# A selective-scan block with a feed-forward net: the decay's exponentials taken in one instruction over two PSUM banks

## The chip, the cores and the metric

The kernel runs on one core of one Trainium2 chip. A core has TensorE (PE, matrix products), VectorE (DVE), ScalarE (ACT), GpSimd (POOL) and SyncE (SP, which here issues the DMAs). Each engine works through its own queue in order; engines wait for one another by semaphores. TensorE writes its products to PSUM, which has eight banks of 2 KB per partition (512 float32 columns each).

The metric is the device time of one execution in microseconds (us), lower is better. The kernel before takes 2990.38 us, the median of three runs (2989.24 to 2991.91).

## The reference

x is (2, 1024, 512). A selective state-space layer with state size 128 for each of the 512 channels, a residual and a layernorm, then a gated feed-forward net of width 2048, a residual and a layernorm. Cut to what matters:

```python
xn = x * rsqrt(mean(x * x, -1) + 1e-06) * norm_w
xn = xn * sigmoid((xn @ select_proj_w.T + select_proj_b) * select_gate)
delta, B_ssm, C_ssm = split(xn @ x_proj_w.T)            # 128 each
delta = softplus(delta @ dt_proj_w.T + dt_proj_b)
A = -exp(A_log)                                          # (512, 128)
def step(h, inp):                                        # over 1024 tokens
    dt, bt, ct, xt = inp
    h = exp(dt[:, :, None] * A) * h + (dt * xt)[:, :, None] * bt[:, None, :]
    return h, einsum('bdn,bn->bd', h, ct)
x = layernorm(x + (ys + x * D_param) @ out_proj_w.T)
x = layernorm(x + (silu(x @ w_gate.T) * (x @ w_up.T)) @ w_down.T)
```

The recurrence over tokens is the core of it: for each token, channel and state a decay exp(dt A) and an input dt x B.

## The kernel before, in words

**Tiling.** The 2048 tokens are cut into 64 groups of 32 tokens (`st`). In each, the 512 channels are done in two halves (`h = 2 st + i`, 128 of them), and each half in eight rounds (`r`, lines 636 to 698) of 32 channels. So there are 1024 rounds `k`. States lie on the 128 partitions. A round's tile is 128 x 32 x 32: 32 channels of 32 tokens each, 1024 columns, two PSUM banks.

**One round.** TensorE makes two tiles with four matmuls, each with a contraction of 32 rows that stand in a quarter of the array of its own:

- `bu` (line 658, two matmuls, one bank each): the products dt x B of round k. The pool `ps_bu` has two buffers of two banks.
- `a` (line 391, in `decay_mm`, two matmuls): the exponents dt A, made one round ahead, for round k + 1. Each matmul has a tile of one bank, and the pool `ps_a` has two of them. They are issued alternately with those of `bu`: bu, a, bu, a.

ScalarE takes the exp of the exponents into `a_sb` (line 398, in `decay_exp`), for columns 1 to 31 of each channel, so 16 x 31 = 496 columns for each of the two banks. Column 0 of `a_sb` stays zero; that restarts the scan at each channel. For this ScalarE also copies the state carried over from the group before, with the first token's input added to it, into column 0 of `bu` (line 669, 32 columns; called the first tokens' copy here). `a_sb` holds three rounds.

VectorE runs the recurrence in one scan over the 1024 columns (line 674) from `a_sb` and `bu` into `hs[h]`. The scan needs the exp of its round, which was made one round before, and the copy of its own round.

**The order in a round.** The order of each engine is written out by hand. In a round of the loop: first `work.others()`, which issues what ScalarE, VectorE, GpSimd and SyncE have to do for the layers around the scan; then bu, a, bu, a; then on ScalarE the first exp, the copy, the second exp; then the scan; then what is called TensorE's side group here:

- `y_round` (line 410): products of the states with C for the half before. Rounds 1, 4 and 7 of a half have three, three and two of these, by the list `ROUNDS` (line 21).
- `work.tensor()`: one step of a generator for the next tokens' projections (`pre`), the output projection (`post`) or the feed-forward net (`ffn`). A step is mostly one matmul 128 x 256 with a contraction of 128. The list `PARTS` (line 22) gives each round a credit of 4, 3 or none; unused credit is kept up to 6. If no step is ready in the written order, `work.tensor()` returns False and the side group of that round ends there.

So the length of the side groups varies, and it is fixed when the program is built. After the side group GpSimd gets the next inputs of the matmuls (`diag`, lines 362 and 372) and the parts of the carried state (`carry_a`, `carry_h`).

**What waits for what around the change.** The matmul of `a` in round k + 1 writes the bank that an exp of round k reads, so it waits for this exp. `bu` of round k + 2 uses the banks of `bu` of round k, so it waits for scan k. TensorE's queue is in order: what is behind a waiting matmul waits too.

Of the kernel before, what the change touches and what calls it, by code (L numbers as in the profile page):

```python
# [9 lines left out]
FP = mybir.dt.float32  # L10
AF = mybir.ActivationFunctionType
ALU = mybir.AluOpType
PSUM = bass.MemoryType.PSUM
DRAM = bass.MemoryType.DRAM

P = 128
S = 32
# [3 lines left out]
ROUNDS = ((), (0, 1, 2), (), (), (3, 4, 5), (), (), (6, 7))  # L21
PARTS = (4, 0, 3, 3, 0, 3, 3, 0)
# [12 lines left out]
def kernel(  # L35
# [17 lines left out]
    nc = tc.nc  # L53
# [50 lines left out]
    a_t = main.tile([P, NM, N], FP, name="a_t")  # L104
# [7 lines left out]
    a_sb = main.tile([P, 3, 32, S], FP, name="a_sb")  # L112
# [8 lines left out]
    ps_y = tc.alloc_tile_pool(name="ps_y", bufs=1, space=PSUM)  # L121
    ps_m = tc.alloc_tile_pool(name="ps_m", bufs=1, space=PSUM)
    ps_bu = tc.alloc_tile_pool(name="ps_bu", bufs=2, space=PSUM)
    ps_a = tc.alloc_tile_pool(name="ps_a", bufs=2, space=PSUM)

    x_tr = x_t.rearrange("(k p) t -> p k t", p=P)
    first_xT = pre_pool.tile([P, NM, TC], FP, tag="xT", name="xT_0")
# [180 lines left out]
    def toks(st):  # L308
        return ts(st % SPC, S)

    prepared, carried, dus, ddts, hs, ys = {}, {}, {}, {}, {}, {}

    def load(st):


        ub = step_pool.tile([P, 2, P], FP, tag="ub", name=f"ub_{st}")
        rows = u_d[ts(st, S), :].rearrange("t (m g c) -> g t m c", g=4, c=32)
        for g in range(4):
            nc.sync.dma_start(
                ub[ts(g, S), 0, :].rearrange("t (m c) -> t m c", c=32), rows[g]  # L320
            )
            nc.sync.dma_start(ub[ts(g, S), 1, :], b_d[ts(st, S), :])
        prepared[st] = ub
        nc.gpsimd.tensor_copy(
            cz[st % 3][:, 28:284].rearrange("p (b w) -> p b w", w=32)[:, :, 0:4],
            made[st // SPC][2][:, toks(st)].rearrange("p (b t) -> p b t", t=4),
        )
        cd = step_pool.tile([P, D], FP, tag="cd", name=f"cd_{st}")
        cu = step_pool.tile([P, D], FP, tag="cu", name=f"cu_{st}")
        nc.sync.dma_start(cd, dt0_d[st : st + 1, :].to_broadcast([P, D]))  # L330
        nc.sync.dma_start(cu, u_d[st * S : st * S + 1, :].to_broadcast([P, D]))
        carried[st] = cd, cu
# [9 lines left out]
    def carry_h(st, i):  # L342

        if st % NSB == 0:
            return
        cd, cu = (t.rearrange("p (b i e) -> p b i e", i=2, e=16)[:, :, i, :] for t in carried[st])
        last = hs[2 * (st - 1) + i][:, :, S - 1].rearrange("p (b e) -> p b e", e=16)
        nc.gpsimd.tensor_tensor(cd, cd, last, ALU.mult)  # L348
        nc.gpsimd.tensor_tensor(cu, cu, cd, ALU.add)

    def diag(j, part):

        h, a = j // 2, 2 * (j % 2)
        if h >= 2 * NS:
            return
        st, i = divmod(h, 2)
        name, m = divmod(part, 2)
        shape = [P, 2, 16, S]
        if name == 0:
            if m == 0:  # L360
                ddts[j] = half_pool.tile(shape, FP, tag="ddt", name=f"ddt_{j}")
            nc.gpsimd.tensor_tensor(  # L362
                ddts[j][:, m, :, :],
                made[st // SPC][0][:, a + m, toks(st)].unsqueeze(1).to_broadcast([P, 16, S]),
                hot[:, ts(i, 16)].unsqueeze(2).to_broadcast([P, 16, S]),
                ALU.mult,
            )
        else:
            if m == 0:
                dus[j] = half_pool.tile(shape, FP, tag="du", name=f"du_{j}")  # L370
            uv = prepared[st][:, 0, :].rearrange("p (m i e) -> p m i e", i=2, e=16)[:, :, i, :]
            nc.gpsimd.tensor_tensor(  # L372
                dus[j][:, m, :, :],
                uv[:, a + m, :].unsqueeze(2).to_broadcast([P, 16, S]),
                hot.unsqueeze(1).to_broadcast([P, 16, S]),
                ALU.mult,
            )

    NG = NS * 16

    def place(k):
        h, r = divmod(k, 8)
        m, pair = divmod(r, 2)
        return h, m, pair

    def decay_mm(k, b):

        h, m, pair = place(k)
        g = 2 * pair + b
        ps = ps_a.tile([P, 16, S], FP, tag="a", name=f"a_{k}_{b}")  # L390
        nc.tensor.matmul(  # L391
            ps, a_t[ts(g, 32), m, :], ddts[k // 4][ts(g, 32), m % 2, :, :],
            start=True, stop=True,
        )
        return ps

    def decay_exp(k, b, ps):
        nc.scalar.activation(  # L398
            a_sb[:, k % 3, ts(b, 16), 1:], ps[:, :, 1:], AF.Exp
        )  # L400

    def y_round(h, b):


        st, i = divmod(h, 2)
        if i == 0 and b == 0:
            ys[st] = ps_y.tile([P, 512], FP, tag="y", name=f"y_{st}")
        at = 28 + 28 * b
        for m in range(NM):
            nc.tensor.matmul(  # L410
                ys[st][ts(m, 32), ts(i, 256)], cz[st % 3][:, at : at + 32],
                hs[h][:, ts(m, 64), ts(b, 4)],
                start=(i == 0 and b == 0), stop=(i == 1 and b == 7),
                skip_group_check=True,
            )

    def y_out(st):

        tt, s = divmod(st, 4)
        if s == 0:  # L420
            yrs[tt] = post_pool.tile([P, 4, P], FP, tag="yr", name=f"yr_{tt}")
        yc = post_pool.tile([P, P, 4], FP, tag="yc", name=f"yc_{st}")
        nc.scalar.copy(yc, ys.pop(st).rearrange("p (q t) -> p q t", t=4))  # L423
        nc.gpsimd.tensor_tensor(yc, yc, pick.unsqueeze(1).to_broadcast([P, P, 4]), ALU.mult)  # L424
        nc.gpsimd.tensor_tensor(yc[:, :, 0:2], yc[:, :, 0:2], yc[:, :, 2:4], ALU.add)
        nc.gpsimd.tensor_tensor(yrs[tt][:, s, :], yc[:, :, 0], yc[:, :, 1], ALU.add)
        if s == 3:
            work.add(post(tt), front=True)
# [191 lines left out]
    work = Work()  # L620
# [8 lines left out]
    for part in range(4):  # L629
        diag(0, part)  # L630
    diag(1, 0)
    for b in range(2):
        decay_exp(0, b, decay_mm(0, b))

    pres, credit = {}, 0
    for k in range(NG):
        h, m, pair = place(k)
        st, i = divmod(h, 2)
        r = k % 8
        work.others()  # L640
        if r == 0:
            hs[h] = half_pool.tile([P, 256, S], FP, tag="h", name=f"h_{h}")

            if i == 1 and st:
                y_out(st - 1)
            if i == 0:
                if st % SPC == 0 and st // SPC + 1 < NC:
                    pres[st // SPC + 1] = work.add(pre(st // SPC + 1), front=True)
                if st + 1 < NS:
                    if (st + 1) % SPC == 0:  # L650
                        work.finish(pres[(st + 1) // SPC])
                    load(st + 1)

        bu = ps_bu.tile([P, 32, S], FP, tag="bu", name=f"bu_{k}")
        nxt = []
        for b in range(2):
            g = 2 * pair + b
            nc.tensor.matmul(  # L658
                bu[:, ts(b, 16), :], prepared[st][ts(g, 32), 1, :],
                dus[k // 4][ts(g, 32), m % 2, :, :],  # L660
                start=True, stop=True,
            )
            if k + 1 < NG:
                nxt.append(decay_mm(k + 1, b))
        if nxt:
            decay_exp(k + 1, 0, nxt[0])
        h0 = carried[st][1].rearrange("p (b i e) -> p b i e", i=2, e=16)
        first = 4 * m + 2 * pair
        nc.scalar.copy(  # L669
            bu[:, :, 0].rearrange("p (b e) -> p b e", e=16), h0[:, first : first + 2, i, :]  # L670
        )
        if nxt:
            decay_exp(k + 1, 1, nxt[1])
        nc.vector.tensor_tensor_scan(  # L674
            hs[h][:, ts(r, 32), :].rearrange("p q t -> p (q t)"),
            a_sb[:, k % 3, :, :].rearrange("p q t -> p (q t)"),
            bu.rearrange("p q t -> p (q t)"),
            0.0, ALU.mult, ALU.add,
        )
        if h:  # L680
            for b in ROUNDS[r]:
                y_round(h - 1, b)
        credit = min(credit + PARTS[r], 6)
        while PARTS[r] and credit > 0 and work.tensor():
            credit -= 1

        j, r4 = divmod(k, 4)
        if r4 == 3:
            diag(j + 2, 0)
        else:  # L690
            diag(j + 1, r4 + 1)
        if r == 1:
            if i == 0 and st:
                carry_h(st, 1)
            if i == 1 and st + 1 < NS:
                carry_h(st + 1, 0)
        if r == 5 and i == 0 and st + 1 < NS:
            carry_a(st + 1)
# [81 lines left out]
```

## Time and profile before

| | |
|---|---|
| median of three runs | 2990.38 us |
| the profiled execution | 2998.38 us, its span 2996.6 us |
| mean granted TensorE clock | 0.973 of full speed |
| TensorE busy | 2808.5 us (94%) |
| VectorE busy | 2370.2 us (79%), 2313.3 of it in 1024 scans |
| ScalarE busy | 1697.1 us (57%), 1206.3 of it in 2048 exps of line 398 |
| GpSimd busy | 1928.4 us (64%) |
| DMA | 171.89 MB, 18.2% of 16 engines' span for the main queue |
| the loop of 1024 rounds | from about 92 to 2880 us of the span |

The profile is one execution. Busy time of TensorE counts matmuls, which overlap: the four of a round run together. The chain that ended last follows the work back from the last instruction, at each step to what released it. An entry in the table of waits says which engine, at which line, stood idle until which other instruction ended: total us, times, the longest. In the timeline the columns are the start in us from the start of the span, the duration, the engine, the line, the operation and its tiles. Each float32 matmul appears as two records, one behind the other.

### The profile page before, as it was taken

What the parts mean: (1) busy time and instruction counts of PE and PEld (TensorE: products, weight loads), DVE (VectorE), ACT (ScalarE), POOL (GpSimd) and SP (SyncE); (2) the same over time, 40 slices, a digit from 0 to 9 for tenths busy, and PEclk for the clock granted to TensorE, in tenths of its full rate; (3) what the DMA queues carried; (4) which work ended last, traced back from release to release, by engine and by line L of the source; (5) the groups of instructions that cost most, each with busy time, mean ns of one, the idle gap of its engine ahead of it and who ended that gap; (6) DMA issues with size and microseconds to landing.
All of it is one profiled execution on the core that took longest, in us unless ns stands there. A gap on an engine that the chain in (4) does not pass through costs nothing.

```text
span 2996.6 us, 53059 instructions
## 1 busy us (share of the span) xinstructions
PE 2808.5 (94%) x20672; PEld 1422.4 (47%) x20672; DVE 2370.2 (79%) x1184; ACT 1697.1 (57%) x4139; POOL 1928.4 (64%) x2094
## 2 busy tenths in 40 slices
PE   3798889999999999999999999999999999999988
PEld 2333334444444444444444444445444445454457
DVE  0589998888778888888888878888888888988840
ACT  2465566656465566665656546565656656565633
POOL 2465665767657676775666656767676757675734
PEclk7799999999999999999999999999999999999999
DMA  1101011212112121112202112111211212122124
GB/s 62 38 19 25 18 32 56 60 61 67 46 54 61 53 66 57 53 51 82 68 29 65 61 52 74 42 54 58 88 48 40 82 57 62 61 68 67 59 78 120
DMA packets 119673, 171.89 MB, mean 57 GB/s; under 512 B 47808, under 2 KB 70848, under 8 KB 119424
## 3 DMA queue, kind: packets, MB, share of 16 engines
q1 hardware_dynamic: 119424, 168.50, 18.2%
q8 instruction: 165, 2.70, 0.4%
q14 instruction: 84, 0.69, 0.1%
HBM read 158.87 MB, written 9.57 MB: 56 GB/s over the span
## 4 chain that ended last, share of the span: by engine, by line
PE 74%; DVE 13%; ACT 5%; issue 4%; POOL 3%; DMA 1%; SPq 0%; POOLq 0%; ACTq 0%; DVEq 0%
PE bu L658 26%; PE gu L514 15%; PE y L410 14%; DVE h L674 12%; PE d L532 7%; PE a L391 6%; PE op L457 2%; PE sel L181 2%; PE xp L181 1%; ACT a_sb L398 1%; ACT bu L669 1%; PE ss L195 1%; PE b L241 1%; POOL du L372 0%; POOL dt L305 0%
## 5 line engine op out<-in xcount | busy, mean ns | idle before, releaser
L674 DVE TENSOR_TENSOR_SCAN h<-a_sb,bu 128x1024 f32<-128x1024 f32 x1024 | 2313.3, 2280 | 520.3 <-ACT bu L669 515.0
L398 ACT ACTIVATE a_sb<-a 128x496 f32<-128x496 f32 x2048 | 1206.3, 591 | 1021.1 <-PE a L391 848.4
L391 PE MATMUL a<-ddt,a_t 32*128 32x512 f32 x4096 | 1307.1, 649 | 14.4 <-POOL ddt L362 13.4
L658 PE MATMUL bu<-du,ub 32*128 32x512 f32 x4096 | 1205.1, 647 | 49.8 <-DVE h L674 44.5
L362 POOL TENSOR_TENSOR ddt<-dt,hot 128x512 f32<-128x512 f32 x512 | 533.3, 1048 | 281.1 <-PE a L391 281.0
L372 POOL TENSOR_TENSOR du<-ub,hot 128x512 f32<-128x512 f32 x512 | 534.5, 1049 | 46.5 <-PE a L391 46.0
L658 PEld LDWEIGHTS bu<-du,ub 32*128 32x128 f32 x4096 | 338.7, 185 | 454.5 <-issue 280.9
L514 PE MATMUL gu<-x1T,w 128*128 128x256 f32 x2048 | 525.4, 399 | 20.2 <-DMA w<-in_wgu_s_dram 4.9
L410 PE MATMUL y<-h,cz 128*32 128x256 f32 x8192 | 530.5, 388 | 1.6 <-DVE h L674 1.6
L514 PEld LDWEIGHTS gu<-x1T,w 128*128 128x128 f32 x2048 | 373.3, 193 | 271.3 <-issue 183.1
L391 PEld LDWEIGHTS a<-ddt,a_t 32*128 32x128 f32 x4096 | 410.6, 185 | 56.0 <-ACT a_sb L398 34.2
L410 PEld LDWEIGHTS y<-h,cz 128*32 128x32 f32 x8192 | 229.5, 110 | 414.6 <-issue 304.3
L548 POOL TENSOR_SCALAR gu<-gu 128x256 f32<-128x256 f32 x128 | 108.4, 847 | 301.5 <-ACT gu L520 301.1
L532 PE MATMUL d<-w,hid 128*128 128x256 f32 x1024 | 260.9, 396 | 14.7 <-DVE x L538 6.9
L532 PEld LDWEIGHTS d<-w,hid 128*128 128x128 f32 x1024 | 185.0, 191 | 138.8 <-issue 98.5
L669 ACT COPY bu<-cu 128x32 f32<-128x32 f32 x1024 | 200.5, 196 | 1.4 <-PE bu L658 1.4
L424 POOL TENSOR_TENSOR yc<-yc,pick 128x512 f32<-128x512 f32 x64 | 66.5, 1039 | 165.4 <-ACT yc L423 165.4
L348 POOL TENSOR_TENSOR cd<-cd,h 128x256 f32<-128x256 f32 x124 | 106.4, 858 | 62.4 <-DVE h L674 62.4
L554 POOL TENSOR_TENSOR hid<-gu,e 128x256 f32<-128x256 f32 x128 | 93.0, 727 | 30.3 <-ACT e L553 27.9
L549 POOL TENSOR_TENSOR gu<-gu 128x256 f32<-128x256 f32 x128 | 94.3, 736 | 10.7
L520 ACT COPY gu<-gu 128x512 f32<-128x512 f32 x128 | 75.0, 586 | 45.8 <-PE gu L514 45.7
L538 DVE TENSOR_TENSOR x<-x,d 128x256 f32<-128x256 f32 x64 | 25.5, 399 | 94.9 <-PE d L532 94.9
(91 smaller groups left out, 1446.4 us busy)
## 6 DMA issues: line engine op xcount, KB each, us to landing
w<-in_wgu_s_dram SPq DMA_DIRECT2D x128, 512.0 KB, 4.6
w<-in_wd_s_dram SPq DMA_DIRECT2D x64, 512.0 KB, 4.1
cd<-dt_d SPq DMA_DIRECT2D x64, 256.0 KB, 3.8
cu<-u_d SPq DMA_DIRECT2D x64, 256.0 KB, 4.8
xT<-in_x_t_dram SPq DMA_DIRECT2D x8, 512.0 KB, 5.3
u_d<-uT SPq DMA_DIRECT2D x16, 256.0 KB, 2.0
ub<-u_d SPq DMA_DIRECT2D x256, 16.0 KB, 2.1
ub<-b_d SPq DMA_DIRECT2D x256, 16.0 KB, 1.9
```

Of the source, the lines that this page charges most:

```text
L348: nc.gpsimd.tensor_tensor(cd, cd, last, ALU.mult)
L362: nc.gpsimd.tensor_tensor(ddts[j][:, m, :, :], made[st // SPC][0][:, a + m, toks(st)].unsqueeze(1).to_broadcast([P, 16, S]), hot[:, ts(i, ...
L372: nc.gpsimd.tensor_tensor(dus[j][:, m, :, :], uv[:, a + m, :].unsqueeze(2).to_broadcast([P, 16, S]), hot.unsqueeze(1).to_broadcast([P, 16, ...
L391: nc.tensor.matmul(ps, a_t[ts(g, 32), m, :], ddts[k // 4][ts(g, 32), m % 2, :, :], start=True, stop=True,)
L398: nc.scalar.activation(a_sb[:, k % 3, ts(b, 16), 1:], ps[:, :, 1:], AF.Exp)
L410: nc.tensor.matmul(ys[st][ts(m, 32), ts(i, 256)], cz[st % 3][:, at : at + 32], hs[h][:, ts(m, 64), ts(b, 4)], start=(i == 0 and b == 0), s ...
L514: nc.tensor.matmul(ps[:, ts(a, TC)], w[:, a, k, :], x1T[:, k, :], start=(k == 0), stop=(k == NM - 1),)
L532: nc.tensor.matmul(ps[:, 0:HD], hid[:, f, ts(j, P)], w[:, f % 4, :], start=(f == 0), stop=(f == NH - 1),)
L548: nc.gpsimd.tensor_scalar_max(g, g, -80.0)
L658: nc.tensor.matmul(bu[:, ts(b, 16), :], prepared[st][ts(g, 32), 1, :], dus[k // 4][ts(g, 32), m % 2, :, :], start=True, stop=True,)
L669: nc.scalar.copy(bu[:, :, 0].rearrange("p (b e) -> p b e", e=16), h0[:, first : first + 2, i, :])
L674: nc.vector.tensor_tensor_scan(hs[h][:, ts(r, 32), :].rearrange("p q t -> p (q t)"), a_sb[:, k % 3, :, :].rearrange("p q t -> p (q t)"), b ...
```

## The change

The exponents `a` of a round come in one tile of two banks, and `ps_a` has one such tile instead of two of one bank: the same two banks. One exp of 32 x 31 = 992 columns takes the place of two of 496. Since it reads both banks, both matmuls of `a` of the next round wait for it.

The side group is now written ahead of the exp, the copy and the scan in the program, so that its length is known there; on TensorE's own queue the order stays. `size` counts its y rounds and its steps. With `size` below 3 the exp is issued ahead of the first tokens' copy, otherwise behind it.

```diff
-    ps_a = tc.alloc_tile_pool(name="ps_a", bufs=2, space=PSUM)
+    ps_a = tc.alloc_tile_pool(name="ps_a", bufs=1, space=PSUM)
...
-    def decay_mm(k, b):
+    def decay_mm(k, b, ps):
...
-        ps = ps_a.tile([P, 16, S], FP, tag="a", name=f"a_{k}_{b}")
         nc.tensor.matmul(
-            ps, a_t[ts(g, 32), m, :], ddts[k // 4][ts(g, 32), m % 2, :, :],
+            ps[:, ts(b, 16), :], a_t[ts(g, 32), m, :], ddts[k // 4][ts(g, 32), m % 2, :, :],
             start=True, stop=True,
         )
-        return ps
-
-    def decay_exp(k, b, ps):
-        nc.scalar.activation(
-            a_sb[:, k % 3, ts(b, 16), 1:], ps[:, :, 1:], AF.Exp
-        )
+
+    def decay_exp(k, ps):
+        nc.scalar.activation(a_sb[:, k % 3, :, 1:], ps[:, :, 1:], AF.Exp)
+
+    def decay_bank(k):
+        return ps_a.tile([P, 32, S], FP, tag="a", name=f"a_{k}")
...
-        nxt = []
+        nxt = decay_bank(k + 1) if k + 1 < NG else None
...
-            if k + 1 < NG:
-                nxt.append(decay_mm(k + 1, b))
-        if nxt:
-            decay_exp(k + 1, 0, nxt[0])
+            if nxt is not None:
+                decay_mm(k + 1, b, nxt)
+
+        size = 0
+        if h:
+            for b in ROUNDS[r]:
+                y_round(h - 1, b)
+                size += 1
+        credit = min(credit + PARTS[r], 6)
+        while PARTS[r] and credit > 0 and work.tensor():
+            credit -= 1
+            size += 1
+
+        if nxt is not None and size < 3:
+            decay_exp(k + 1, nxt)
         h0 = carried[st][1].rearrange("p (b i e) -> p b i e", i=2, e=16)
         first = 4 * m + 2 * pair
         nc.scalar.copy(
             bu[:, :, 0].rearrange("p (b e) -> p b e", e=16), h0[:, first : first + 2, i, :]
         )
-        if nxt:
-            decay_exp(k + 1, 1, nxt[1])
+        if nxt is not None and size >= 3:
+            decay_exp(k + 1, nxt)
         nc.vector.tensor_tensor_scan(
...
-        if h:
-            for b in ROUNDS[r]:
-                y_round(h - 1, b)
-        credit = min(credit + PARTS[r], 6)
-        while PARTS[r] and credit > 0 and work.tensor():
-            credit -= 1
```

More of the change, by code (lines that the diff above doesn't have):

```diff
@@ L631 @@
     diag(1, 0)
+    ps = decay_bank(0)
     for b in range(2):
-        decay_exp(0, b, decay_mm(0, b))
+        decay_mm(0, b, ps)
+    decay_exp(0, ps)
     pres, credit = {}, 0
```

## The prediction

> **What bounds the kernel now.** I read the page first: the busy shares and the chain that ended last.
>
> ```profile
> PE 2808.5 (94%) x20672; PEld 1422.4 (47%) x20672; DVE 2370.2 (79%) x1184; ACT 1697.1 (57%) x4139; POOL 1928.4 (64%) x2094
> ...
> PE 74%; DVE 13%; ACT 5%; issue 4%; POOL 3%; DMA 1%; SPq 0%; POOLq 0%; ACTq 0%; DVEq 0%
> ```
>
> TensorE carries three quarters of the chain, and ScalarE, whose instructions the change rewrites, one twentieth. So only that part of the change counts that lets TensorE start something sooner or later. Next the groups by line, for the three instruction kinds that move or set the moves:
>
> ```profile
> L674 DVE TENSOR_TENSOR_SCAN h<-a_sb,bu 128x1024 f32<-128x1024 f32 x1024 | 2313.3, 2280 | 520.3 <-ACT bu L669 515.0
> L398 ACT ACTIVATE a_sb<-a 128x496 f32<-128x496 f32 x2048 | 1206.3, 591 | 1021.1 <-PE a L391 848.4
> ...
> L669 ACT COPY bu<-cu 128x32 f32<-128x32 f32 x1024 | 200.5, 196 | 1.4 <-PE bu L658 1.4
> ```
>
> One scan, two exps and one copy per round, 1024 rounds. Then the table of waits:
>
> ```profile
> ACT a_sb L398 <- PE a L391: 848.4, 593, 9.5
> DVE h L674 <- ACT bu L669: 515.0, 603, 96.4
> ...
> PEld a L391 <- ACT a_sb L398: 34.2, 124, 1.0
> ```
>
> ScalarE mostly waits for TensorE, so its idle time is no cost. In 603 rounds VectorE stands idle until the first tokens' copy: the copy's place matters to the scan. The last line shows TensorE waiting for an exp, but only 34 us, because it counts a wait only while nothing else runs in TensorE. The timeline shows the rest. Here are a round with two y rounds as its side group, a round with two small steps, and the start of the next; columns are start, duration, engine, line:
>
> ```profile
> 1172.51 0.69 PE L658 MATMUL bu<-du,ub 32*128 32x512 f32 x1
> ...
> 1173.58 1.07 PE L410 MATMUL y<-h,cz 128*32 128x256 f32 x16
> 1173.71 0.60 ACT L398 ACTIVATE a_sb<-a 128x496 f32<-128x496 f32 x1 [4.64 <-PE a L391]
> ...
> 1174.20 0.20 ACT L669 COPY bu<-cu 128x32 f32<-128x32 f32 x1
> 1174.30 0.60 ACT L398 ACTIVATE a_sb<-a 128x496 f32<-128x496 f32 x1
> 1174.43 4.46 DVE L674 TENSOR_TENSOR_SCAN h<-a_sb,bu 128x1024 f32<-128x1024 f32 x2 [2.56 <-ACT bu L669]
> 1174.59 0.69 PE L658 MATMUL bu<-du,ub 32*128 32x512 f32 x1
> 1174.60 0.69 PE L391 MATMUL a<-ddt,a_t 32*128 32x512 f32 x1
> 1174.60 0.69 PE L658 MATMUL bu<-du,ub 32*128 32x512 f32 x1
> 1174.95 0.69 PE L391 MATMUL a<-ddt,a_t 32*128 32x512 f32 x1
> ...
> 1175.79 0.58 ACT L398 ACTIVATE a_sb<-a 128x496 f32<-128x496 f32 x1 [0.89 <-PE bu L658]
> 1176.01 1.13 PE L457 MATMUL op<-out_w,zT 128*128 128x256 f32 x4
> 1176.27 0.19 ACT L669 COPY bu<-cu 128x32 f32<-128x32 f32 x1
> 1176.38 0.59 ACT L398 ACTIVATE a_sb<-a 128x496 f32<-128x496 f32 x1
> ...
> 1177.07 0.69 PE L658 MATMUL bu<-du,ub 32*128 32x512 f32 x1
> ```
>
> A round starts with four matmuls (bu, a, bu, a) that run side by side within 20 ns of each other. The fourth of the second round does not: it starts at 1174.95, 0.36 late, 0.05 after the second exp of the round before ended (1174.30 + 0.60). Everything behind it on TensorE, here the op steps at 1176.01, is late by as much. Walking the timeline round by round, I find the last exp to be what TensorE waits for in 370 rounds, 206 us together (late fourth matmul plus late first one). That is the sum the change can work on. It sits in rounds after a short side group. I counted each round's units from the matmuls in it (one y round is 8 records, most steps are 2): 404 rounds have under three units, 126 of them the eighth round of a half with its two y rounds. They lie in 248 runs: 139 alone, 79 pairs, 30 longer ones. After a side group of three or more the exps are long done (in the usual round they end 2.38 after the round's start, and the next starts at 2.51 to 2.56).
>
> **What the Trainium skill says.** "ScalarE: Activation LUTs", section "What ACT_TABLE_LOAD costs", prices an activation with constant scale and bias at 186 ns plus 0.833 ns a column, and lets neighbours overlap by 93 ns. The trace agrees: 496 columns give 599 by that against 591 measured, and the copy starts 0.48 to 0.49 after an exp of 0.59, an overlap of about 0.11. "PSUM — Partial Sum Buffer", section "PSUM bank collisions raise a hardware error", wants two engines kept off one bank at once; hence each decay matmul waits for the exp that reads its bank, as at 1174.95. "TensorEngine Tiling (Array Packing)", section "Key Properties", has row tiles run independently: the four starts within 20 ns show it.
>
> **The change part by part.**
>
> *Two exps of 496 become one of 992.* Exps of 256 and 512 columns in the groups by line take 416 and 628 ns, so 0.83 ns a column; 587 (the usual duration of an L398) + 496 x 0.83 = 1.00 us. The skill's formula gives an estimate of 1.01. No row shows an exp across two banks: the ends I keep are 0.97 and 1.04.
>
> *Both decay matmuls now wait for that one exp.* Before, the first half's bank came free with the first exp. Now bu(0) starts and a, bu, a follow the exp. As the fourth matmul was the last anyway, a late exp costs the side group no more than before; where the exp was early it costs nothing. But the exp itself now needs the whole of a delayed four: it starts 1.21 after the delayed start, where the first exp of 1175.79 came 1.20 after the undelayed one (1174.59).
>
> *Long side group (at least three units): copy, then exp.* Copy at 1.20 after the start, exp from 1.31 to 2.31; before, 2.38. Nothing in TensorE waits for it at 2.51 and later. The scan can start 0.48 earlier, at 1.43 instead of 1.91, which is hidden by VectorE's slack (79% busy): price nothing; were that cover gone it would be a gain, since earlier scans free bu sooner.
>
> *Short side group: exp, then copy.* Exp from 1.21 to 2.21, so 0.165 ahead of 2.38 for the first round of a run. In the example: exp 1173.72 to 1174.72, the late matmuls at 1174.77 or so, op at 1175.84 instead of 1176.01. This holds for the 246 first rounds in the loop's steady part: 246 x 0.165 = 40.6 us gained.
>
> But the copy then ends 0.09 after the exp, at 2.30 instead of 1.88, and queued behind it is this round's scan. In 230 of those 246 rounds the scan started right on its copy (about 0.03 after it), so it becomes 0.42 later. Who waits for it: bu of the next but one round, which takes the same pair of banks (two bu buffers). In the example scan one would run 1174.85 to 1177.13, and bu starts 0.055 to 0.147 after a scan's end where it waits for one: 1177.23 in place of 1177.07. So a pair is not 0.17 ahead but 0.16 behind; its second round gave back 0.33. With an empty second group, the old limit was the second exp's end, 2.38 + 2.07 + 0.05 = 4.50 after the first start (2.07 from start to start); the new one is 2.30 + 0.03 + 2.29 + 0.10 = 4.72, so 0.22 behind, 0.38 given back. Where the second group has two full steps and the first was longer than 2.07, part is covered; there I put 0.23. Mean taken: 0.30 over 107 second rounds, 32 us lost; with the two ends, 25 to 41.
>
> *Third and later rounds of a run (44).* VectorE's 2.29 a round and the new loop exp, matmuls, exp (0.05 + 1.21 + 1.00 = 2.26) are near equal: nothing, with plus or minus 4 us.
>
> *Rest.* Rounds with a wide side group but a late ScalarE (silu, copies) get 0.07 or so sooner results; the waits of TensorE for ScalarE inside side groups number some 40 (gu, sel, z, x1T in the waits), 40 x 0.07 = 3 us at most; taken 1. A first matmul that now waits where it did not: 2 us lost. No DMA, no GpSimd instruction and no SyncE issue moves; in program order the side group comes ahead of exp and copy, but on TensorE the order is the same, and these steps put nothing in ScalarE's queue.
>
> Sum: -40.6 + 32 - 1 + 2 = -7.6. The profiled execution took 2998.4 (span 2996.6), which gives 2991; the median is 8 lower, so 2990.4 - 7.6, rounded 2983.
>
> **Rivals.**
> *Full gain*: the second rounds lose little, because VectorE's slack ahead of them takes the late scan. For it: the 206 us of waits. Against it: the first scans start on their copies. It would give -40 + 5: 2952 to 2973.
> *No measurable change*: seconds lose 0.38; sum 0, 2985 to 2996. Runs and pairs are so evenly matched that this is close behind.
> *Slower*: one mechanism, the copy behind a one-microsecond exp. If the exp takes 1.04, the firsts gain only 0.125 (31 us) and each second round loses 0.38 + 0.04 + 0.04 (exp in both rounds of the loop), 49 us: 18 lost, about 3008. It decides from the point where a second round gives back over 40.6/107 = 0.38.
> That the change does not do what it says would be the exp always on one side of the copy; the rule in the diff is fixed while the program is built, so I give that nothing.
>
> **How the numbers follow.** Forecast (2974 to 2984) 0.36, full gain 0.12, no change 0.32, slower (2997 to 3010) 0.20. A difference below 0.2%, 6 us, can't be told from none here. Faster 0.48, same 0.32, slower 0.20. The range 2966 to 3000 leaves out most of the full gain and the far end of the slower case.
>
> **What would show it.** L398 with half the count and about 1.00 us; fourth matmuls never apart from the second ones; after a lone short group the next side group 0.17 sooner; VectorE's wait for the copy longer in short rounds, shorter in long ones; TensorE waiting for scans (90 + 45 us in the waits before) more, for exps less. Wrong if the exp is not near 1.00, if scans after short rounds are no later, or if pairs lose nothing.

## The result, and the profile after

The changed kernel takes 3036.61 us, the median of four runs (3034.31 to 3039.45), against 2989.81 before: a ratio of 1.0156, with a 95% interval of 1.0138 to 1.0173. It is slower by 47 us, where 7 us faster was forecast, and lies above the range of 2966 to 3000. Its profiled execution took 3034.31 (span 3032.5), 36 more than the profiled one of before (2998.38), which was itself 8 above its median; so the working below accounts for 36 of the 47 us. The profiled execution of before had a granted TensorE clock of 0.973, where 39 later executions of that kernel had 0.974 to 0.979, and an execution at a lower clock is longer (one kernel below took 2981.00 us at 0.980 and 3002.74 at 0.971), so the pair of profiles shows less than the whole loss.

The page of the changed kernel, busy times and the chain that ended last:

```profile
PE 2772.0 (91%) x20672; PEld 1382.4 (46%) x20672; DVE 2362.5 (78%) x1184; ACT 1634.9 (54%) x3115; POOL 1931.6 (64%) x2094
...
PE 73%; DVE 10%; ACT 7%; issue 5%; POOL 3%; DMA 1%; SPq 0%; POOLq 0%; ACTq 0%; DVEq 0%
```

ScalarE has 1024 instructions fewer and 62 us less work, as the change says, and the kernel is slower: less work on this engine saved nothing. TensorE's busy share fell from 94% to 91%. The same three groups by line:

```profile
L686 DVE TENSOR_TENSOR_SCAN h<-a_sb,bu 128x1024 f32<-128x1024 f32 x1024 | 2305.6, 2278 | 563.8 <-ACT bu L681 559.3
...
L396 ACT ACTIVATE a_sb<-a 128x992 f32<-128x992 f32 x1024 | 1025.9, 1002 | 509.0 <-PE a L390 505.1
...
L681 ACT COPY bu<-cu 128x32 f32<-128x32 f32 x1024 | 195.9, 191 | 617.0 <-PE a L390 601.5
```

The exp of 992 columns takes 1002 ns, as priced. VectorE waits longer for the copy, 559 us for 515. In the waits of the changed kernel (total us, times, longest; PE and PEld are the matmul and the weight-load row of one queue) see what TensorE waits for:

```profile
PEld bu L659 <- DVE h L686: 153.5, 166, 2.4
PE bu L659 <- DVE h L686: 98.7, 134, 1.6
...
PEld a L390 <- ACT a_sb L396: 27.2, 54, 1.5
...
PEld d L531 <- DVE x L537: 15.6, 7, 2.4
...
PEld op L456 <- DVE zT L447: 15.2, 11, 2.7
```

and the same waits in the kernel before, but for that on the exp, shown with the prediction:

```profile
PEld bu L658 <- DVE h L674: 91.4, 120, 2.1
PE bu L658 <- DVE h L674: 44.5, 70, 1.3
...
PEld d L532 <- DVE x L538: 12.7, 7, 1.8
...
PEld op L457 <- DVE zT L448: 8.2, 4, 2.1
```

The waits for exps went from 34 to 27 us; the waits for scans rose from 91 and 45 to 154 and 99. One wait of TensorE can stand in both rows, so the two are not added: the PEld row rose by 62 us. The last two lines are a third kind: an output-projection or feed-forward step that waits for an add on VectorE; this add stands in VectorE's queue behind the scans. They are few (7 and 11 waits), and they cost more now.

Here is the pair of short rounds of the prediction (the same rounds of the program), in the timeline of the changed kernel:

```profile
1195.36 0.69 PE L659 MATMUL bu<-du,ub 32*128 32x512 f32 x1
...
1196.60 1.02 ACT L396 ACTIVATE a_sb<-a 128x992 f32<-128x992 f32 x1 [4.72 <-PE a L390]
...
1197.44 0.69 PE L659 MATMUL bu<-du,ub 32*128 32x512 f32 x1
1197.51 0.20 ACT L681 COPY bu<-cu 128x32 f32<-128x32 f32 x1
1197.67 0.69 PE L390 MATMUL a<-ddt,a_t 32*128 32x512 f32 x1
1197.67 0.69 PE L659 MATMUL bu<-du,ub 32*128 32x512 f32 x1
...
1197.74 4.55 DVE L686 TENSOR_TENSOR_SCAN h<-a_sb,bu 128x1024 f32<-128x1024 f32 x2 [3.02 <-ACT bu L681]
...
1198.73 1.13 PE L456 MATMUL op<-out_w,zT 128*128 128x256 f32 x4
...
1200.08 0.69 PE L659 MATMUL bu<-du,ub 32*128 32x512 f32 x1 [0.22 <-DVE h L686]
```

From the first round's start, op comes after 3.37 us (3.50 before): 0.13 gained by the shorter exp. The scan comes after 2.38 (1.92 before), and the next round but one after 4.72 (4.56 before): 0.16 lost over the pair, bu having waited for the scan. In the second round the first bu starts at 1197.44; the second bu stands behind a matmul of a that waits for the exp, and starts with it, at 1197.67. The prediction gave 0.17 gained for the first round, and the same 0.16 lost for the pair.

### The profile page after: what moved, and what is told of

Its sections match the earlier page's. It is cut to its first block, busy times and chain, and to the rows that moved or that the text cites. A ratio compares the mean times of both kernels' runs of the same rounds, so it can differ in the third digit from the quotient of the medians.

```text
span 3032.5 us, 51724 instructions
## 1 busy us (share of the span) xinstructions
PE 2772.0 (91%) x20672; PEld 1382.4 (46%) x20672; DVE 2362.5 (78%) x1184; ACT 1634.9 (54%) x3115; POOL 1931.6 (64%) x2094
## 3 DMA queue, kind: packets, MB, share of 16 engines
q1 hardware_dynamic: 119424, 168.50, 17.7%
## 4 chain that ended last, share of the span: by engine, by line
PE 73%; DVE 10%; ACT 7%; issue 5%; POOL 3%; DMA 1%; SPq 0%; POOLq 0%; ACTq 0%; DVEq 0%
PE bu L659 28%; PE gu L513 15%; PE y L409 13%; DVE h L686 10%; PE d L531 7%; PE a L390 4%; ACT a_sb L396 3%; PE op L456 2%; PE sel L181 1%; PE xp L181 1%; ACT bu L681 1%; POOL dt L305 1%; PE b L241 1%; PE ss L195 1%; POOL du L372 0%
## 5 line engine op out<-in xcount | busy, mean ns | idle before, releaser
L659 PE MATMUL bu<-du,ub 32*128 32x512 f32 x4096 | 1289.5, 651 | 107.1 <-DVE h L686 98.7
L396 ACT ACTIVATE a_sb<-a 128x992 f32<-128x992 f32 x1024 | 1025.9, 1002 | 509.0 <-PE a L390 505.1
L390 PE MATMUL a<-ddt,a_t 32*128 32x512 f32 x4096 | 1186.7, 652 | 18.7 <-POOL ddt L362 13.6
L659 PEld LDWEIGHTS bu<-du,ub 32*128 32x128 f32 x4096 | 392.0, 186 | 516.9 <-issue 258.2
L390 PEld LDWEIGHTS a<-ddt,a_t 32*128 32x128 f32 x4096 | 321.7, 186 | 54.5 <-ACT a_sb L396 27.2
```

What stands on the lines that cost most here:

```text
L390: nc.tensor.matmul(ps[:, ts(b, 16), :], a_t[ts(g, 32), m, :], ddts[k // 4][ts(g, 32), m % 2, :, :], start=True, stop=True,)
L396: nc.scalar.activation(a_sb[:, k % 3, :, 1:], ps[:, :, 1:], AF.Exp)
L659: nc.tensor.matmul(bu[:, ts(b, 16), :], prepared[st][ts(g, 32), 1, :], dus[k // 4][ts(g, 32), m % 2, :, :], start=True, stop=True,)
```

## Where the 36 us are

I went through the timelines round by round. A round is the four matmuls (1.14 us when they start together), TensorE's stall on or among these four, and the side group with whatever it waits for inside. Stalls are grouped by the round before them: long (three units or more), first in a run of short rounds, second, later. In a few cases it is hard to say where a stall ends and a side group begins; another way of cutting there moved the differences between two rows by up to 3 us. All are sums over the loop, in us; the same table holds the experiments below.

| kernel | after long | after first | after second | after later | side groups | loop |
|---|---|---|---|---|---|---|
| before | 13.7 | 124.2 | 45.9 | 28.3 | 1396.7 | 2774.1 |
| after | 17.8 | 103.4 | 78.5 | 32.3 | 1413.0 | 2810.3 |
| e1_copy_first | 16.4 | 122.3 | 71.7 | 34.9 | 1381.8 | 2793.0 |
| e3_two_exps | 19.6 | 96.3 | 80.4 | 34.4 | 1412.7 | 2808.5 |
| e4_one_tile | 17.7 | 142.1 | 80.5 | 37.0 | 1390.9 | 2834.3 |
| e5_two_copy_first | 13.0 | 134.0 | 45.8 | 28.1 | 1372.1 | 2759.0 |
| e7_two_bu_ahead | 12.1 | 118.2 | 41.4 | 27.5 | 1369.5 | 2734.4 |
| e8_one_bu_ahead | 15.0 | 114.6 | 58.2 | 30.5 | 1381.5 | 2765.5 |
| e9_after_bu_ahead | 14.3 | 100.7 | 77.9 | 31.8 | 1407.6 | 2797.6 |

From before to after: -20.8 after first rounds, +32.6 after second ones, +4.0 after later ones, +4.1 after long ones, +16.3 in side groups: +36.2. Each row is one execution, so a few us in it mean little.

The loss is not spread evenly. The first eighth of the loop, rounds 3 to 127, has y rounds in its side groups and little else (63 of 125 side groups are empty): the feed-forward net has no tokens yet. There 88 of 128 rounds are short, against 309 of the other 895. In the rounds of this part VectorE is busy for 89% of the time before (281 of 317 us), where the whole execution has 79%. Split at round 128:

| before to after, us | after long | after first | after second | after later | side groups | loop |
|---|---|---|---|---|---|---|
| rounds 3 to 127 | +1.5 | -2.1 | +16.2 | +2.6 | +4.5 | +22.9 |
| rounds 128 to 1022 | +2.2 | -19.2 | +19.5 | -0.6 | +11.6 | +13.5 |

So most of the loss falls in an eighth of the rounds. In the rest, first and second rounds cancel out, and the side groups make up the loss.

The granted clock has a part in it. The page shows it in 40 slices of the span, in tenths of full speed; first the kernel before, then the changed one:

```profile
PEclk7799999999999999999999999999999999999999
...
PEclk8788999999999999999999999999999999999999
```

In the trace the clock is either full or half, the half for stretches of 3.4 to 10 us in the loop. A y matmul, mostly 0.38 us long, took 0.63 in them. In the first eighth before has 38 us of such stretches, the changed kernel 68; in the rest 48 and 44. At half speed TensorE can lose at most half of such a stretch, so I estimate the clock's part in the 36 us at up to 14. It is mixed up with the stalls: in the first eighth the stretches stand right behind rounds in which TensorE waited. What brings them on was not tried by a run of its own.

## The experiments

Two theories of the loss. A: the copy behind the exp in short rounds makes the scan late, and with it bu two rounds on and VectorE's adds. B: the coupling, since both decay matmuls of a round wait for one exp that itself waits for all four, so that the exps of a run of short rounds follow each other more slowly. A third, C, came up after the first runs. No kernel leaves out any of the computation. The code below is cut to what an edit comes to. Each ratio is to the kernel before, run again beside it.

**One exp, the copy always first.** This takes the late copy out and leaves the coupling.

```diff
-        if nxt is not None and size < 3:
-            decay_exp(k + 1, nxt)
...
-        if nxt is not None and size >= 3:
+        if nxt is not None:
             decay_exp(k + 1, nxt)
```

> The changed kernel with the first tokens' copy ahead of the one exp in every round. Theory A (the loss is the copy behind the exp in short rounds, whose scans come late): no scan is late any more, so the 116 us that TensorE newly waits for scans go; the exp ends at 1.23 + 0.11 + 1.00 = 2.34 after a round's start instead of 2.24, so short rounds gain nothing over the kernel before: 2980 to 3005 us. Theory B (the loss is the coupling: both decay matmuls wait for one exp, which waits for all four matmuls, so that in a run of short rounds one round needs 0.05 + 1.23 + 1.00 us or more where before it took 2.07): the loop gets 0.11 longer still, 3035 to 3060.

Measured: 3020.66 us, ratio 1.0098 (1.0082 to 1.0114). Its waits:

```profile
PEld bu L659 <- DVE h L686: 68.2, 107, 1.7
PEld a L390 <- ACT a_sb L396: 67.5, 120, 1.7
...
PE bu L659 <- DVE h L686: 13.5, 47, 0.8
```

That is between both expectations, and within neither. The waits for scans are now below those of before, and the side groups are 15 us shorter than before: what A says of late scans holds (its 116 us add two rows that share waits). But the waits for exps have doubled, and after second rounds TensorE still stalls 71.7 us for 45.9: with the late copy gone, the coupling keeps the same groups of four matmuls waiting.

**One exp, always first.**

```diff
-        if nxt is not None and size < 3:
+        if nxt is not None:
             decay_exp(k + 1, nxt)
...
-        if nxt is not None and size >= 3:
-            decay_exp(k + 1, nxt)
```

> The changed kernel with the one exp ahead of the copy in every round. Theory A: the long rounds' scans come late too (0.42 us against the kernel before), which adds waits for scans where a short round follows, and delays what is queued behind scans on VectorE: 3040 to 3070 us. Theory B: the exp is no later anywhere, so as the changed kernel, 3030 to 3040.

Measured: 3038.87 us, 1.0154 (1.0132 to 1.0177), as the changed kernel and as B had it. Putting the copy first in long rounds was worth nothing there. After a round's start the scan of a long round comes 2.04 us in the changed kernel (median), no earlier than before (1.92); with the exp first everywhere it comes after 2.38, and with the copy first everywhere after 1.47. So in the changed kernel the early copy of a long round does not make its scan early. That VectorE is still working off the late scans of short rounds would explain it, as the scans do come early where short rounds have the copy first too; it is read from these medians. A missed: it expected a loss from later scans in long rounds; they came 0.34 later than in the changed kernel, and that cost nothing.

**Two tiles, two exps, the changed order.** This leaves the late copy and takes the coupling out.

```diff
-    ps_a = tc.alloc_tile_pool(name="ps_a", bufs=1, space=PSUM)
+    ps_a = tc.alloc_tile_pool(name="ps_a", bufs=2, space=PSUM)
...
-            ps[:, ts(b, 16), :], a_t[ts(g, 32), m, :], ddts[k // 4][ts(g, 32), m % 2, :, :],
+            ps[b], a_t[ts(g, 32), m, :], ddts[k // 4][ts(g, 32), m % 2, :, :],
...
-        nc.scalar.activation(a_sb[:, k % 3, :, 1:], ps[:, :, 1:], AF.Exp)
+        for b in range(2):
+            nc.scalar.activation(a_sb[:, k % 3, ts(b, 16), 1:], ps[b][:, :, 1:], AF.Exp)
...
-        return ps_a.tile([P, 32, S], FP, tag="a", name=f"a_{k}")
+        return [ps_a.tile([P, 16, S], FP, tag="a", name=f"a_{k}_{b}") for b in range(2)]
```

> The order of the changed kernel (side group first in the program, both exps ahead of the copy in short rounds, behind it in long ones), but with two tiles of one bank and two exps of 496. Theory A: in short rounds the copy stands behind both exps, 1.07 us after the first one's start, about as late as in the changed kernel: 3020 to 3045 us. Theory B: each decay matmul has its own bank and exp again: 2975 to 2995.

Measured: 3043.01 us, 1.0167 (1.0141 to 1.0192), as A has it (the profiled execution was the fastest, 3031.95). TensorE stalls 28 us less after first rounds than before, and the whole loss is still there:

```profile
PEld bu L660 <- DVE h L687: 151.3, 165, 2.4
PE bu L660 <- DVE h L687: 101.7, 131, 1.6
...
PEld a L390 <- ACT a_sb L397: 17.6, 68, 0.8
```

The waits for scans are those of the changed kernel. So the order alone, the copy behind the exps in short rounds, is enough for a loss of this size.

**One tile, two exps, the order of before.** This has the coupling alone: one tile of two banks, with exp, copy, exp as before. The edit is against the kernel before.

```diff
-    ps_a = tc.alloc_tile_pool(name="ps_a", bufs=2, space=PSUM)
+    ps_a = tc.alloc_tile_pool(name="ps_a", bufs=1, space=PSUM)
...
-        ps = ps_a.tile([P, 16, S], FP, tag="a", name=f"a_{k}_{b}")
...
-            ps, a_t[ts(g, 32), m, :], ddts[k // 4][ts(g, 32), m % 2, :, :],
+            ps[:, ts(b, 16), :], a_t[ts(g, 32), m, :], ddts[k // 4][ts(g, 32), m % 2, :, :],
...
-            a_sb[:, k % 3, ts(b, 16), 1:], ps[:, :, 1:], AF.Exp
+            a_sb[:, k % 3, ts(b, 16), 1:], ps[:, ts(b, 16), 1:], AF.Exp
...
+    def decay_bank(k):
+        return ps_a.tile([P, 32, S], FP, tag="a", name=f"a_{k}")
```

> The kernel before (exp, copy, exp of 496, each on half), but with the two banks in one tile: both decay matmuls of a round wait for the second exp of the round before, and the first exp waits for both matmuls. Theory A: the scan is as early as before, and the fourth matmul waited for the second exp anyway: 2985 to 3005 us. Theory B: the loop of a run of short rounds gets 0.05 + 1.23 + 0.48 + 0.11 + 0.59 = 2.46 us long: 3030 to 3070.

Measured: 3058.71 us, 1.0224 (1.0207 to 1.0240), as B has it; A's expectation is far off. The waits for scans are near those of before:

```profile
PEld bu L662 <- DVE h L678: 97.6, 134, 1.8
...
PEld a L390 <- ACT a_sb L396: 51.3, 114, 1.3
...
PE bu L662 <- DVE h L678: 35.4, 57, 1.0
```

The stall after first rounds is 18 us more than before, after second ones 35 more. So the coupling alone costs as well. Here it costs more than the whole change; the single exp of the change is shorter than the sequence of exp, copy and exp. The two causes do not add up: taking out either one leaves a loss.

**Two tiles, two exps, the copy always first.** The changed form with neither cause. The edit is that of the third kernel, with the order of the first: behind the copy, in every round, stands a `decay_exp` of two exps of 496.

```diff
+        if nxt is not None:
+            decay_exp(k + 1, nxt)
```

> Two tiles of one bank and two exps of 496 as before, the copy ahead of both in every round. The exps' ends stay at 1.90 and 2.38 after a round's start (first one 0.11 later than before), the scan starts 0.48 earlier. Theory A (late scans cost, early scans give): the waits of TensorE for scans, 136 us in the kernel before, fall, and VectorE's adds come sooner: 2965 to 2982 us. Theory B (only the exps' chain counts): same as before, 2985 to 3000, as the first exp is later and the second where it was.

Measured: 2988.68 us, 0.9997 (0.9981 to 1.0014), the time of before, as B had it. With neither cause the loss is gone. A had expected a gain: the side groups did get 25 us shorter in the profiled execution (2982.5 us, 6 faster than the median), but the first exp is 0.11 later, and after first rounds 10 us are given back. The kernel with the changed order differs from this one in the place of the copy alone, and its side groups are 41 us longer.

**The same only in long rounds.** Short rounds keep exp, copy, exp.

```diff
+        if nxt is not None and size < 3:
+            decay_exp(k + 1, nxt, (0,))
...
+        if nxt is not None:
+            decay_exp(k + 1, nxt, (1,) if size < 3 else (0, 1))
```

> The kernel before (two tiles, exp, copy, exp), but in rounds with a side group of three or more the copy ahead of both exps. Theory A: a short round begins with less of a queue at VectorE, so part of the gain of early scans: 2972 to 2988 us. Theory B: no exp is later or earlier where TensorE waits for it: 2987 to 2994.

Measured: 2993.09 us, 1.0011 (1.0003 to 1.0020), as B had it. No gain: an earlier scan in long rounds alone is worth nothing to the whole, as the prediction had priced it.

Theory C: the matmuls stand in the queue as bu, a, bu, a. Where the first a waits for an exp, the second bu stands behind it, and behind that bu the copy and the scan. Then the order bu, bu, a, a should help.

**Two exps, the copy first, bu ahead.**

```diff
-            if nxt is not None:
-                decay_mm(k + 1, b, nxt)
+        if nxt is not None:
+            for b in range(2):
+                decay_mm(k + 1, b, nxt)
```

> As the run with two exps and the copy first, and the four matmuls in the order bu, bu, a, a, so that the second bu never stands behind a decay matmul that waits for an exp. Theory A: in short rounds the copy and the scan come sooner yet: 5 to 20 us below that run. Theory B: the last decay matmul still waits for the second exp, so no different from that run by more than 5 us.

Measured: 2959.82 us (2959.16 to 2960.64), ratio 0.9898 (0.9882 to 0.9913): 1% faster than the kernel before, 2.5% than the changed one. It is 29 us below the run with the old order of the matmuls: more than A's 5 to 20, and against B, which saw no difference. The pair of rounds again, in its timeline:

```profile
1152.68 0.70 PE L660 MATMUL bu<-du,ub 32*128 32x512 f32 x2
...
1153.86 0.19 ACT L683 COPY bu<-cu 128x32 f32<-128x32 f32 x1 [4.13 <-PE a L390]
...
1154.08 4.46 DVE L688 TENSOR_TENSOR_SCAN h<-a_sb,bu 128x1024 f32<-128x1024 f32 x2 [2.04 <-ACT bu L683]
...
1154.76 0.70 PE L660 MATMUL bu<-du,ub 32*128 32x512 f32 x2
1154.77 1.02 PE L390 MATMUL a<-ddt,a_t 32*128 32x512 f32 x2
...
1156.15 1.13 PE L457 MATMUL op<-out_w,zT 128*128 128x256 f32 x4
...
1157.21 0.70 PE L660 MATMUL bu<-du,ub 32*128 32x512 f32 x2
```

Both bu of a round start together, and the copy does not depend on an exp. The scan starts 1.40 after the round (1.92 before), and the round after the pair 4.53 (4.56 before).

**One exp, the copy first, bu ahead.** The same edit to the first kernel of this section.

> One tile and one exp of 992, the copy first in every round (3021 us in that form), and the four matmuls in the order bu, bu, a, a. Theory A: what is left of the loss there was the second bu, and with it the copy and the scan, behind a waiting decay matmul: 2985 to 3005 us. Theory B: the loop exp, matmuls, copy, exp of 0.05 + 1.23 + 0.11 + 1.00 = 2.39 us in runs of short rounds is the loss, and the new order leaves it, or takes at most the copy out of it: 3008 to 3022.

Measured: 2988.80 us, 0.9992 (0.9979 to 1.0005), 32 us below that kernel, within A's expectation, whose text there gives C's reason. But bu ahead gains as much with two tiles, where there is no coupling: 29 us (2988.68 to 2959.82). So it does not take the coupling's cost away. With the copy first the coupling costs 32 us in the old order of the matmuls (3020.66 against 2988.68) and 29 in the new one (2988.80 against 2959.82): so these look like two separate effects of about one size.

**The changed kernel, bu ahead.** The same edit.

> The changed kernel with nothing but the matmuls in the order bu, bu, a, a. Theory A (in short rounds the copy behind the exp makes the scan late): the copy stays behind the exp, so TensorE goes on waiting for scans, about 250 us as in the changed kernel, and the time stays at 3020 to 3038 us. Theory C (the loss is the second bu behind a decay matmul that waits for the exp): as with the copy first in this order, 2985 to 3005.

Measured: 3023.29 us, 1.0104 (1.0078 to 1.0130), within A's expectation. The waits for scans are as in the changed kernel:

```profile
PEld bu L659 <- DVE h L687: 153.3, 168, 2.4
PE bu L659 <- DVE h L687: 99.5, 135, 1.6
...
PEld a L390 <- ACT a_sb L396: 25.3, 53, 1.4
```

This kernel and the one above differ only in the place of the exp in short rounds: 3023 against 2989. With bu ahead, the rule that puts the exp before the copy in short rounds costs 34 us.

**The kernel before, bu ahead**, and **one tile with two exps, bu ahead**: the edit in the two kernels that have exp, copy, exp.

> The kernel before with the matmuls in the order bu, bu, a, a and nothing else. Theory C: the first decay matmul of a round seldom waits there, because the first exp ends at 1.79, so little was lost by the order: 2975 to 2990 us, and the gain of the run with both is that of order and early copy together. If it is the order alone: 2958 to 2968.

> The kernel before with one tile of two banks (3059 us in that form) and the matmuls in the order bu, bu, a, a. Theory B (the loop of exps, 2.46 us in runs of short rounds, is the cost of the coupling): 3040 to 3060 us. Theory C (the coupling costs by the second bu that stands behind the waiting decay matmul): 3000 to 3030.

Measured: 2995.45 us, 1.0006 (0.9994 to 1.0018), a little above the expectation; and 3049.60, 1.0190 (1.0163 to 1.0216), as B has it, with C's expectation missed: where the copy stands behind an exp anyway, freeing the second bu brings little (9 us of 68). With two tiles, copy first alone gives nothing, bu ahead alone gives nothing, and both give 1%: the copy is early only if neither an exp nor a waiting matmul stands before it. That the two need each other in this way is read from the times of these kernels. The clock has a part in this gain too: the profiled execution with both has 41 us of half-clock stretches in the loop, the kernel before 85.

**Where the two causes act.** The kernels split at round 128, in us (one execution each; half clock: the sum of its stretches):

| kernel | rounds 3 to 127 | half clock | rounds 128 to 1022 | half clock |
|---|---|---|---|---|
| before | 317.1 | 38 | 2459.4 | 48 |
| e6_long_copy_first | 312.8 | 27 | 2454.8 | 38 |
| after | 340.0 | 68 | 2472.9 | 44 |
| e1_copy_first | 343.0 | 72 | 2452.6 | 31 |
| e3_two_exps | 334.3 | 55 | 2476.6 | 51 |
| e5_two_copy_first | 312.6 | 24 | 2449.0 | 38 |
| e7_two_bu_ahead | 303.4 | 14 | 2433.4 | 27 |
| e8_one_bu_ahead | 331.9 | 58 | 2436.3 | 27 |
| e9_after_bu_ahead | 333.3 | 55 | 2466.7 | 44 |

The second row has the time of before, so the first two show how far one execution can be trusted. The coupling (e1 against e5, e8 against e7) costs 30.4 and 28.5 us in the first eighth, and 3.6 and 2.9 in all the rest. The late copy (e3 against e5, both with two tiles) costs 22 in the first eighth and 28 in the rest. The changed kernel has both: in the rest it loses by the late copy (20 us more than e1), and in the first eighth it is about as slow as with the coupling alone. So there either cause is enough, and they do not add up. With one tile and bu ahead it is the same: the late copy (e9 against e8) costs 1 us in the first eighth and 30 in the rest. But the coupling brings 44 to 48 us more of half-clock stretches in the first eighth, which can be up to 24 of its 30 us; how much of the cost is the clock and how much the longer loop stays open.

## Why the prediction was wrong

Two steps failed. The gain of the first short rounds came out at half of what was taken. And the late scan was charged to bu alone, where it also holds up steps of the side groups. A third, the coupling taken as free, is paid for in the first eighth of the loop. The sum was -40.6 + 32 - 1 + 2. Term by term:

- *First short rounds, 246 x 0.165 = 40.6.* Mis-sized: 20.8. The exp ends 2.23 after the round's start, not 2.21, since it starts at 1.233, behind the last of four matmuls; 0.14 ahead of before, and the matmuls behind it need 0.02 more to follow one another. In 176 of the rounds the next matmul starts 0.053 after the exp, and the mean gain is 0.11. In 69 it has a second wait, for a newly made ddt, starts 0.144 after the exp, and the gain is 0.03. Before, only the fourth matmul was late, and it had one wait. In the first eighth of the loop the 31 first rounds gained almost nothing (2 us).
- *Second rounds, 107 x 0.30 = 32.* The sum was right: 32.6, and the example to 0.01. In part this is luck. The 30 in the first eighth lose 0.54 each, over the largest loss allowed (0.38), and the other 77 lose 0.25.
- *Later rounds, nothing.* 4.0, the end of the range that was kept.
- *Long rounds, "hidden by VectorE's slack (79% busy): price nothing".* The price was near: 4.1 (and 2 for first matmuls that newly wait). The premise did not hold: the scans of long rounds did not come 0.48 earlier. And 79% is the mean of the whole execution, where VectorE is busy for 89% of the first eighth of the loop.
- *Rest, -1.* This step failed in its sign: side groups take 16.3 more. The prediction asked who waits for a late scan and named bu alone; it did not ask what is queued behind the scan on VectorE. There the adds of the output projection and the feed-forward net stand, and steps of the side groups wait for them. Groups of such steps are 10 us longer. Another 5 are y groups, of which 17 and not 11 ran in half-clock stretches. The two kernels with two tiles whose copies alone differ in place (41 us in the side groups) show that it is the scan's place that moves this.
- *The exp itself, 0.97 to 1.04.* Right: 1.002.

So 36 us instead of -7.6, with 20 of the difference from the first rounds, 17 from the side groups, and the rest from long and later rounds. The first rounds alone, with half of their gain, would have turned the forecast into a loss of some 12.

The rival called slower named one right mechanism, the copy behind a one-microsecond exp, with the wrong point of decision: it did not need an exp of 1.04. The range failed because the gain of a first round was tied to the exp's length alone.

The coupling was priced as free in the prediction ("a late exp costs the side group no more than before"). That holds for a first round. For runs of short rounds the prediction did work out the loop of exp and matmuls, 2.26, and held it level with VectorE's 2.29. The runs show otherwise: with the late copy taken out, the coupling costs about 30 us, nearly all in the first eighth of the loop. The mean of the whole loop hid this part, in which TensorE has little else to do than these rounds. The clock's half-speed stretches, which become longer there, were in no term of the sum.

## What to carry to other kernels

When an edit moves an instruction that releases a long operation of another engine, list everything in that engine's queue behind this operation, not only its direct reader. Fewer, larger instructions on ScalarE, which was 57% busy, saved nothing here by themselves, and they joined buffers that had been released one by one. Split a long loop into stages before using a mean: an eighth of the rounds held more than half of the loss. In an in-order queue, put the instruction that others wait for ahead of the one that itself waits: here bu, bu, a, a with the copy first gave 1%, and each half of that, without the other, gave nothing.

## What the runs showed of the hardware

One activation across two PSUM banks took 1002 ns for 992 columns, as much as the estimate from activations on one bank (1.00 us); no cost of the second bank is seen. A matmul that waits for one exp started 0.053 us after its end (176 rounds). One that has a wait on a second semaphore as well started 0.144 to 0.145 after it (69 rounds), however long before that other wait was over: about 0.09 for the second wait. A matmul that waits in TensorE's queue held up one of another quarter of the array behind it: in the changed kernel's timeline the second bu starts at 1197.67 with the matmul of a before it, 0.23 after the first bu. In half-clock stretches a y matmul took 0.63 us and not 0.38.
